# First self attention of a two-layer decoder: output products of tile pairs by seven block products in place of eight

## The chip, the cores and the metric

The kernel runs on one core of a Trainium2 chip. Its time is the device time of one execution in microseconds (us). All matmuls that matter here are in fp32; in the traces each of them shows as two rows of TensorE, each with its own weight load. TensorE is called PE below, VectorE DVE, ScalarE ACT, GpSimd POOL, as the profile does.

## The reference

The input is 8 sequences of 112 tokens of width 512, that is 896 tokens or 7 token tiles of 128. Two decoder layers follow each other, each with self attention, cross attention and a feed-forward part, each behind a layer norm and added to the residual stream `x`. The part that matters is the self attention of the first layer:

```python
q = (x @ Wq + bq).reshape(Bq, Tq, H, D)      # H = 32 heads of D = 64
k = (x @ Wk + bk).reshape(Bq, Tq, KV, D)     # KV = 8
v = (x @ Wv + bv).reshape(Bq, Tq, KV, D)
q = q * cos + _rotate_half(q) * sin          # k likewise
scores = einsum('bhqd,bhkd->bhqk', q, k) * D ** (-0.5)   # causal, window of 64
combined = concatenate([scores, sink_col], axis=-1)
probs = softmax(combined, axis=-1)[..., :-1]
out = einsum('bhqk,bhkd->bhqd', probs, v).reshape(Bq, Tq, H * D)
return out @ Wo + bo
```

The change is in the last product, `out @ Wo`, with `out` of 896 x 2048 and `Wo` of 2048 x 512. The second layer's self attention has the same shape of output product.

## The kernel before

**Turns and units.** `self_attention(layer)` serves both layers. The 2048 rows of `Wo` are four groups `g` of 512 (8 heads of 64 in the first layer); the 8 sequences are two halves `hf` of 4. A turn is one group and one half, in the order of `turns` (turn n is group n // 2, half n % 2). In the first layer a turn has 4 units, one sequence each.

**The pipeline.** `pipeline` runs a turn in two stretches: `weave` mixes the main steps of two units with filler steps, in proportion to their listed costs. The main steps of a unit are two transposes of probabilities (`ppt`), the scores of the unit two ahead (`ps`) and the context product (`po`, written to `oT` by ACT). The first stretch's filler is the preparation of the next turn (`prepare`: one k and four q projections, `pr_k` and `pr_q`, each rotated by `roped`) and the late output products of the turn before. The second stretch's filler is the early output products of this turn and extra steps (biases and the sums of absolute values for the feed-forward weights, `ternary_sum`, L1108). PE's order is the order in which the program emits; it is fixed by hand (`manual_schedule`). The order on the other engines is planned when the kernel is built: of the instructions that are ready, the one earliest in the program goes first. Each engine then works through its own queue in that order and stops at an instruction whose input is missing.

**The output products.** A token tile can be projected when all its tokens have passed `oT`; `completed` says which: of half 0 early tile 0, late tiles 1 and 2; of half 1 early tiles 3 and 4, late tiles 5 and 6. `project_out` runs 4 matmuls of 128 x 512 outputs into one bank of PSUM (`po_at`, L442 and L446) and DVE adds the bank to `x` (L447).

**The seven products.** In the second layer, and there for groups 0 to 2, `outputs` gives a pair of tiles to `out_pair` instead. It takes the product of [2 token tiles x 2 halves of the group's rows] by [2 halves of rows x 2 halves of columns] as a 2 x 2 block product with 7 block products in place of 8 (Strassen's scheme in Winograd's form): each block product is 2 matmuls of 256 columns. `lay` makes the sums of the weight blocks for a group (`wos`, partly in place in the weights; lines 267 to 272), `add_up` those of `oT` (`os`, and one block of `oT` in place; L253 to L258). `sevens` runs the products in the order 1, 6, 2 (`first`) and 5, 7, 3, 4 (`second`) through two banks of PSUM: product 2 is accumulated onto product 1's bank, 3 onto 5's and 4 onto 7's, and between them `put` copies or adds the bank out with DVE into `od` (L768, L771):

```python
        def first():
            ...
            product(1, "x")
            product(6, "y")
            product(2, "x")

        def second():
            ...
            product(5, "y")
            product(7, "z")
            product(3, "y")
            product(4, "z")
```

Two adds into `x` are POOL's (L782, L785). `wos`, `os` and `od` have one buffer each.

**The softmax beside it.** Each unit's scores go through DVE (mask add L463, negated maximum L466), ACT (8 exponentials L469), DVE (reciprocal L472) and POOL (L476). POOL also copies the sinks in (L461). A rotated q takes ACT (bias), two transfers on SP's queue (`turned_q`), POOL (L639), DVE (L640) and POOL (L641).

Of the kernel before, what the change touches and what calls it, by code (L numbers as in the profile page):

```python
# [24 lines left out]
G = 4  # L25
# [68 lines left out]
def _spans(widths):  # L94
    at, out = 0, {}
    for k, n in widths.items():
        out[k] = (at, n)
        at += n
    return out, at
# [58 lines left out]
def decoder(ctx: ExitStack, tc: tile.TileContext, i: dict, out: bass.AP):  # L158
# [9 lines left out]
    def stage_pool(name, side="left"):  # L168

        return tc.alloc_tile_pool(name=name, bufs=2, side=side, reuse_waits="tile")  # L170
# [14 lines left out]
    def weight(src, name, pool=None, tag="w", bufs=None, behind=None):  # L185
        t = (pool or wpool).tile([P, 4, D], F32, tag=tag, bufs=bufs, name=name)
        fetch(t.rearrange("p a b -> p (a b)"), src, behind)
        return t
# [8 lines left out]
    spans, n = _spans(_COLS)  # L197
# [7 lines left out]
    rspans, n = _spans(_ROWS)  # L205
# [12 lines left out]
    def col(name, k):  # L218
        return cols[:, spans[name][0] + k : spans[name][0] + k + 1]
# [55 lines left out]
    def later(steps):  # L275
        return [(0.0, f) for f in steps]
# [109 lines left out]
    def turned_tile(src, xT, k, name, bank=None):  # L386

        pt = (bank or turning)(f"pt_{name}_{k}").rearrange("p (c t) -> p c t", c=NC)
        for c in range(NC):
            nc.tensor.transpose(pt[:, c, :], src[:, c * P : (c + 1) * P], ident)  # L390
        for hf in range(2):
            lo, hi = max(k * P, hf * HT), min((k + 1) * P, (hf + 1) * HT)
            if lo < hi:
                nc.scalar.copy(xT[hf][:, :, lo - hf * HT : hi - hf * HT], pt[:, :, lo - k * P : hi - k * P])
# [20 lines left out]
    def entering(pool, xT, name, tiles, bufs, bank=None):  # L415

        xn = {}

        def norm():
            xn.update(zip(tiles, normed(pool, tiles, name, bufs)))  # L420

        return [(0.0, norm)] + [(0.45, lambda k=k: turned_tile(xn[k], xT, k, name, bank)) for k in tiles]
# [120 lines left out]
    def self_attention(layer, following=None, behind=None, xT=None):  # L543

        l0 = layer == 0
# [5 lines left out]
        dq, wos = [], {}  # L551

        if l0:
            pool, mid, top, tpool = (
                stage_pool("at0"), stage_pool("atm0"), stage_pool("att0"), stage_pool("tern0", "right")
            )
# [23 lines left out]
        else:  # L580
            npool, pool, top = (stage_pool(f"at{t}1", "right") for t in "nmt")
# [6 lines left out]
        def values(b):  # L588
            ps = mm(f"pv{layer}_{b}")
            accumulate(ps[:T, :], [(xT[b // HB][:, c, bcols(b)], wv[:, c, :]) for c in range(NC)])  # L590
            if l0:
                nc.vector.tensor_tensor(v[:, b, :], ps[:T, :], row("bv"), ALU.add)
            else:
                nc.vector.tensor_copy(v[:, b, :], ps[:T, :])
# [26 lines left out]
        def roped(dst, w, at, xh, bias, which, name):  # L621

            cos, sin = (
                const(f"{n}{which}{layer}").unsqueeze(1).to_broadcast([P, HB, T]) for n in ("cos", "sin")
            )
            ps = mm(f"pr_{name}")
            accumulate(ps[:, :HT], [(w[:, c, at : at + P], xh[:, c, :]) for c in range(NC)])
            raw = top.tile([P, HT], F32, tag="raw", bufs=3, name=f"raw_{name}")
            if bias is None:
                nc.vector.tensor_copy(raw, ps[:, :HT])  # L630
            else:
                nc.scalar.activation(raw, ps[:, :HT], AF.Identity, bias=bias)

            turned = top.tile([P, HT], F32, tag="turned", bufs=3, name=f"turned_{name}")
            for at in range(0, P, half):
                other = at ^ half
                issued.append(nc.sync.dma_start(out=turned[at : at + half, :], in_=raw[other : other + half, :]).ins)
            by_batch = lambda t: t.rearrange("p (b t) -> p b t", b=HB)
            nc.gpsimd.tensor_tensor(by_batch(dst), by_batch(raw), cos, ALU.mult)  # L639
            nc.vector.tensor_tensor(by_batch(turned), by_batch(turned), sin, ALU.mult)  # L640
            nc.gpsimd.tensor_tensor(dst, dst, turned, ALU.add)  # L641

        def prepare(n):
            g, hf = turns[n]
            nm = f"{layer}_{g}_{hf}"
            for k in {0: [] if l0 else [0, 1], 1: [0, 1] if l0 else []}.get(n, [g + 1] if hf == 1 and g + 1 < G else []):
                matrices[k] = [
                    wq0 if l0 and m == "q" and k == 0
                    else weight(i[f"{key}_{m}"][k], f"w{m}{layer}_{k}", behind=behind if k == 0 else None)
                    for m in "qo"  # L650
                ]
            wq = wq0 if l0 and g == 0 else matrices[g][0]
            home = mid if hf else top
            kT = home.tile([P, HT], F32, tag="kT", bufs=1, name=f"kT_{nm}")
            qT = home.tile([P, 4, HT], F32, tag="qT", bufs=1, name=f"qT_{nm}")
            held[n].update(kT=kT, qT=qT)
            steps = []
            if l0 and n == 7:
                steps = list(joined[0]["raw"])
            elif n == 1:  # L660
                steps = [(3.4, lambda b=b: values(b)) for b in (2, 3)[1 if l0 else 0 :]]
                if not l0:
                    steps += entering(npool, xT, "at1", [6], 3)
            steps += [(3.0, lambda: roped(kT, wk, g * P, xT[hf], col("bk", g) if l0 else None, "k", f"k_{nm}"))]
            more = later(lay(g - 1)) if not l0 and n and hf == 0 else []
            for c in range(4):
                steps += more[c : c + 1]
                steps.append((3.0, lambda c=c: roped(
                    qT[:, c, :], wq, c * P, xT[hf], col("bq", 4 * g + c) if l0 else None, "q",
                    f"q_{nm}_{c}",  # L670
                )))
            if n == 1:
                steps += [(3.4, lambda b=b: values(b)) for b in (4, 5)]
            if l0 and n == 0:
                for k in range(4, NT):
                    steps.insert(2 * k - 6, (0.45, lambda k=k: turned_tile(xn[k], xT, k, "at0")))
            if l0 and n == 7:
                for k, rope in enumerate(joined[0]["ropes"][:4]):
                    steps.insert(len(steps) - 3 + k, rope)
            return steps  # L680
# [42 lines left out]
        def lay(g):  # L723

            b = matrices[g][1].rearrange("p (h k) (s n) -> p h k s n", h=2, s=2)

            def new():
                wos[g] = dq[0].tile([P, 3, 2, D // 2], F32, tag="wos", bufs=1, name=f"wos_{layer}_{g}")

            return block_differences(  # L730
                (nc.vector, nc.gpsimd), new, lambda k: b[:, 0, :, 1] if k == 2 else wos[g][:, min(k, 2)],
                b[:, 0, :, 0], b[:, 0, :, 1], b[:, 1, :, 0], b[:, 1, :, 1],
            )
# [58 lines left out]
        def outputs(n, late):  # L792
            g, hf = turns[n]
            tiles = completed(hf, late)
            if not l0 and len(tiles) == 2 and g < G - 1:
                return out_pair(g, tiles[0], f"at{layer}_{n}_{late}")
            return [
                (3.4, lambda k=k: project_out(
                    k, [(oT[:, c, k * P : (k + 1) * P], matrices[g][1][:, c, :]) for c in range(4)], f"at{layer}_{n}"
                ))  # L800
                for k in completed(hf, late)
            ]
# [16 lines left out]
        def go():  # L819
            nonlocal oT, late  # L820
            if not l0:
                late = stage_pool("atl1")
                joined.append(following(npool, late))
            if not l0:
                dq.append(stage_pool("dq"))
            oT = (pool if l0 else late).tile([P, 4, NB * T], F32, tag="oT", bufs=1, name=f"oT{layer}")
            pipeline(
                turns, HB if l0 else HB // 2, 2 if l0 else 1, prepare, scores, contexts, outputs, extra,
                begun=None if l0 else 0, finale=finale, between=l0,
                keys_early=(2, 4) if l0 else (),  # L830
            )
            if l0:
                pool.release()
            joined[0]["go"]()
            if not l0:
                for p in (late, pool, npool):
                    p.release()
# [1098 lines left out]
```

## Time and profile before

| | |
|---|---|
| time, median of 3 runs | 1810.11 us (1806.64 to 1810.22) |
| profiled execution | 1806.85 us, span 1804.1 us |
| PE busy | 1758.9 us, 97% |
| DVE busy | 947.0 us, 52% |
| ACT busy | 627.6 us, 35% |
| POOL busy | 799.2 us, 44% |
| 75 to 327 us of the span: PE, DVE, ACT, POOL busy | 251.00, 153.44, 107.46, 132.14 of 252 us |
| granted TensorE clock | 0.999 |

The first self attention's turns lie between about 40 and 345 us of the span. In the lines of the order of time, the first number is the start, the second the length of the merged piece, then engine, line of the source, operation, what is written from what, the shape, and the number of instructions; in brackets stands how long the engine had been idle and what released it. `po_at` is the old projection's bank; `px`, `py` and `pz` are the banks of the seven products; `True` in a name marks a late pair, `False` an early one.

### The profile page before, as it was taken

The numbers are of one execution on the slowest core, as the hardware profiler recorded it, in microseconds if no ns is written. First come the engines' busy times: TensorE is split into PE (matmuls) and PEld (weight loads), VectorE is DVE, ScalarE is ACT, GpSimd is POOL, SyncE is SP. The second block draws the span as 40 slices with busy tenths as digits, with TensorE's granted clock in tenths as the row PEclk, the third lists the DMA queues.
The fourth block names the chain that finished last, engine by engine and source line by source line (L and its number), as shares of the span: only waits on it lengthen the run. The fifth ranks groups of instructions, "written<-read, shape, count | busy, mean of one in ns | idle before, by whom it ended". The sixth has DMA issues, their size and how long they took to land.

```text
span 1804.1 us, 20354 instructions
## 1 busy us (share of the span) xinstructions
PE 1758.9 (97%) x7150; PEld 990.9 (55%) x7150; DVE 947.0 (52%) x1668; ACT 627.6 (35%) x1906; POOL 799.2 (44%) x697
## 2 busy tenths in 40 slices
PE   8999999999999999999999999999999999999998
PEld 4454544555554555567655666655655555555554
DVE  4455666745353544786543455445765444444444
ACT  2444444554333434375321122135733111041110
POOL 3465555355555560000035666621363565535653
PEclk9999999999999999999999999999999999999999
DMA  6132422143223212011221321120011222011101
GB/s 244 27 119 59 148 83 75 76 152 111 53 76 111 59 47 100 19 75 47 70 66 33 86 73 36 39 96 1 2 44 51 60 75 82 24 51 56 63 34 41
DMA packets 40429, 124.50 MB, mean 69 GB/s; under 512 B 7332, under 2 KB 20700, under 8 KB 32904
## 3 DMA queue, kind: packets, MB, share of 16 engines
q1 hardware_dynamic: 33192, 93.73, 16.1%
q0 software_dynamic: 6848, 29.36, 5.5%
q8 instruction: 56, 0.92, 0.2%
q14 instruction: 45, 0.37, 0.1%
q10 hardware_dynamic: 288, 0.12, 0.0%
HBM read 94.56 MB, written 10.28 MB: 58 GB/s over the span
## 4 chain that ended last, share of the span: by engine, by line
PE 87%; DVE 6%; ACT 3%; POOL 1%; SPq 1%; DMA 1%; issue 1%; ACTq 0%; POOLq 0%; DVEq 0%
PE pr_q L244 10%; PE pf L244 6%; PE pb_dn L1550 4%; PE po_x L1004 4%; PE pb_up L1550 4%; PE po_at L442 3%; PE pv L244 3%; PE po_at L446 3%; PE ps L695 3%; PE pr_k L244 3%; PE pq_x L244 3%; PE po L714 3%; PE pg_dn L1550 3%; PE po_x L442 2%; PE po_x L446 2%; PE pg_up L1550 2%
## 5 line engine op out<-in xcount | busy, mean ns | idle before, releaser
L244 PE MATMUL pr_q<-xT_at,wq 128*128 128x448 f32 x512 | 204.1, 543 | 0.0
L244 PEld LDWEIGHTS pr_q<-xT_at,wq 128*128 128x128 f32 x512 | 93.9, 190 | 84.2 <-issue 81.2
L469 ACT ACTIVATE p<-p,nmax 112x113 f32<-112x113 f32 x256 | 95.8, 376 | 109.5 <-DVE nmax L466 108.6
L476 POOL TENSOR_TENSOR p<-p,total 112x896 f32<-112x896 f32 (+1 forms) x56 | 85.3, 1529 | 94.6 <-DVE total L472 87.4
L1736 POOL TENSOR_TENSOR h<-silu,h 128x448 f32<-128x448 f32 x64 | 73.0, 1144 | 95.9 <-ACT silu L1734 95.9
L1127 POOL TENSOR_SCALAR tl<-tr,ternary_bounds 128x512 f32<-128x512 f32 x32 | 51.3, 1603 | 123.3 <-DMA tr<-in_c_w_dram 123.3
L244 PE MATMUL pf<-h,sw 128*128 128x448 f32 x256 | 105.9, 540 | 0.0
L974 DVE TENSOR_REDUCE nmax_x<-ps_x 112x2 f32<-112x750 f32 x64 | 57.2, 934 | 79.1 <-PE ps_x L968 79.1
L639 POOL TENSOR_TENSOR qT<-raw_q,tables 128x448 f32<-128x448 f32 x64 | 86.1, 1350 | 28.0 <-DVE raw_q L630 20.5
L641 POOL TENSOR_TENSOR qT<-qT,turned_q 128x448 f32<-128x448 f32 x64 | 75.2, 1177 | 50.6 <-DVE turned_q L640 41.2
L1004 PE MATMUL po_x<-pT_x,kv 125*128 125x448 f32 x192 | 89.2, 549 | 1.2 <-DVE pT_x L999 0.8
L1550 PE MATMUL pb_dn<-h,sums_dn 128*128 128x448 f32 x192 | 80.2, 540 | 3.4 <-DVE xT_ff L1779 1.7
L976 ACT ACTIVATE p_x<-ps_x,nmax_x 112x375 f32<-112x375 f32 x124 | 69.7, 574 | 38.2 <-DVE nmax_x L974 38.1
L1734 ACT ACTIVATE silu<-pf,cols 128x448 f32<-128x448 f32 x64 | 40.5, 634 | 115.6 <-PE pf L244 114.6
L488 DVE COPY pT<-ppt 112x448 f32<-112x448 f32 x96 | 57.1, 617 | 43.1 <-PE ppt L487 43.0
L469 ACT ACTIVATE p<-ps,nmax 112x112 f32<-112x112 f32 x128 | 43.2, 365 | 102.2 <-DVE nmax L466 102.2
L442 PE MATMUL po_at<-wo,oT 128*128 128x512 f32 x152 | 74.3, 611 | 0.0
L244 PEld LDWEIGHTS pf<-h,sw 128*128 128x128 f32 x256 | 48.5, 190 | 46.5 <-issue 40.1
L446 PE MATMUL po_at<-wo,oT 128*128 128x512 f32 x152 | 71.4, 592 | 0.0
L476 POOL TENSOR_TENSOR p_e<-p_e,total_e 112x896 f32<-112x896 f32 x16 | 26.9, 1682 | 96.5 <-DVE total_e L472 72.2
L719 ACT COPY oT<-po 128x448 f32<-128x448 f32 x64 | 31.9, 524 | 104.8 <-PE po L714 104.8
L995 PEld LDWEIGHTS ppt_x<-consts,p_x 112*125 112x125 f32 x372 | 50.2, 188 | 29.6 <-issue 15.3
(358 smaller groups left out, 3953.7 us busy)
## 6 DMA issues: line engine op xcount, KB each, us to landing
tw<-in_c_w_dram SPq DMA_DIRECT2D x16, 512.0 KB
tr<-in_c_w_dram POOLq DMA_DIRECT2D x32, 256.0 KB, 4.1
signs<-tl POOLq DMA_DIRECT2D x32, 256.0 KB, 2.9
fup<-in_f_up_dram SPq DMA_DIRECT2D x8, 1024.0 KB
fdn<-in_f_dn_dram SPq DMA_DIRECT2D x8, 1024.0 KB
turned_q<-raw_q SPq DMA_DIRECT2D x128, 56.0 KB
turned_q<-raw_q SPq DMA_DIRECT2D x64, 112.0 KB
share<-gated SPq DMA_DIRECT2D x12, 448.0 KB
```

What stands on the lines that cost most here:

```text
L244: nc.tensor.matmul(ps, lhsT, rhs, start=(k == 0), stop=(k == len(pairs) - 1))
L442: nc.tensor.matmul(ps[0], lhsT, rhs, start=(c == 0), stop=False)
L446: nc.tensor.matmul(ps[0], lhsT, rhs, start=False, stop=(c == len(pairs) - 1))
L469: nc.scalar.activation(p[:, h, :], src[:, h, :], AF.Exp, bias=nmax[:, h : h + 1], accum_out=total[:, h : h + 1])
L476: spread[:] = [nc.gpsimd.tensor_tensor(p[:, at, :T], p[:, at, :T], total[:, at], ALU.mult).ins]
L639: nc.gpsimd.tensor_tensor(by_batch(dst), by_batch(raw), cos, ALU.mult)
L641: nc.gpsimd.tensor_tensor(dst, dst, turned, ALU.add)
L974: nc.vector.tensor_reduce(nmax, ps[:T, :, :L], AX.X, ALU.max, negate=True)
L976: e = nc.scalar.activation(p[:, 2 * j + s, :], ps[:T, s, :L], AF.Exp, bias=nmax[:, s : s + 1], accum_out=total[:, 2 * j + s : 2 * j + s + 1],)
L1004: nc.tensor.matmul(po[0][:, : 4 * T], kv[:, b, c, :], pTs[c], start=(c == 0), stop=(c == NLC - 1))
L1550: nc.tensor.matmul(bank[n], lhsT, rhs, start=(k == 0 and n in (1, 6, 7)), stop=(k == len(pairs) - 1), skip_group_check=True,)
L1736: nc.gpsimd.tensor_tensor(to, s, at["h1"][:, c, half(hf)], ALU.mult)
```

## The change

The seven products, so far used in the second layer alone, are used in the first one too: for groups 0, 1 and 2, whenever two tiles come together. `lay` is emitted in the preparation of the next group, `add_up` before the pair's products. The three new tiles `wos`, `os` and `od` lie in the pool `att0` (`top`), which exists in the first layer; group 3 and the single tile 0 of each group are projected as before.

```diff
@@ prepare
-            more = later(lay(g - 1)) if not l0 and n and hf == 0 else []
+            more = later(lay(g - 1)) if n and hf == 0 else []
@@ outputs
-            if not l0 and len(tiles) == 2 and g < G - 1:
+            if len(tiles) == 2 and g < G - 1:
                 return out_pair(g, tiles[0], f"at{layer}_{n}_{late}")
@@ go
-            if not l0:
-                dq.append(stage_pool("dq"))
+            dq.append(top if l0 else stage_pool("dq"))
```

## The prediction

> **What bounds the kernel now.** I read first the busy times on the page, then the chain that ended last, then the order of time on TensorE and VectorE around the projections that the change touches, in the first and in the second self attention.
>
> ```profile
> span 1804.1 us, 20354 instructions
> PE 1758.9 (97%) x7150; PEld 990.9 (55%) x7150; DVE 947.0 (52%) x1668; ACT 627.6 (35%) x1906; POOL 799.2 (44%) x697
> ```
>
> TensorE is the bound. In the windows view the stretch 75 to 327 us, which holds all that changes, has PE busy 251.00 of 252.00 us, VectorE 153.44 and GpSimd 132.14; the chain of waits between 100 and 130 us consists of PE lines alone. So a microsecond of TensorE work taken out there is a microsecond won, and one that TensorE waits is one lost.
>
> What is replaced, and its replacement, both stand in the trace. First, in order of time on PE, two old projections of turn 1 (token tiles 1 and 2):
>
> ```profile
> 108.69 1.04 PE L695 MATMUL ps<-kT,qT 64*112 64x112 f32 x16
> 109.66 1.98 PE L442 MATMUL po_at<-wo,oT 128*128 128x512 f32 x4
> 111.48 1.88 PE L446 MATMUL po_at<-wo,oT 128*128 128x512 f32 x4
> 113.29 0.97 PE L714 MATMUL po<-pT,v 112*64 112x448 f32 x4
> 114.19 1.98 PE L442 MATMUL po_at<-wo,oT 128*128 128x512 f32 x4
> ```
>
> Then a pair of the second self attention, which already uses the seven products (an fp32 matmul shows as two rows, so a product of two matmuls is x4):
>
> ```profile
> 997.82 1.03 PE L286 MATMUL px_at_True<-wo,oT 128*128 128x256 f32 x4
> 998.70 1.13 PE L286 MATMUL py_at_True<-wos,os_at_True 128*128 128x256 f32 x4
> 999.67 1.03 PE L286 MATMUL px_at_True<-wo,oT 128*128 128x256 f32 x4
> ...
> 1003.98 1.74 PE L695 MATMUL ps<-kT,qT 128*112 128x112 f32 x16
> ```
>
> Last, what VectorE does while the first projection of turns 1 and 3 (A pair, then B pair) runs:
>
> ```profile
> 109.78 1.09 DVE L463 TENSOR_TENSOR p<-ps,tables 112x896 f32<-112x896 f32 x1 [0.54 <-PE ps L695]
> 110.78 0.61 DVE L640 TENSOR_TENSOR turned_q<-turned_q,tables 128x448 f32<-128x448 f32 x1
> 111.32 1.09 DVE L466 TENSOR_REDUCE nmax<-p 112x8 f32<-112x904 f32 x1
> ```
>
> ```profile
> 198.97 1.08 DVE L463 TENSOR_TENSOR p<-ps,tables 112x896 f32<-112x896 f32 x1
> 199.97 1.21 DVE L1108 TENSOR_REDUCE ternary_parts<-tw 128x1 f32<-128x1024 f32 x1
> 201.10 1.08 DVE L466 TENSOR_REDUCE nmax<-p 112x8 f32<-112x904 f32 x1
> ```
>
> The planner orders VectorE's queue: whatever is ready goes, earliest in the program first, and a ready instruction slips in between the mask add (L463) and the maximum (L466) that needs it.
>
> **The matmuls (gain).** Nine pairs change: for each of groups 0, 1, 2 one late pair in the odd turn (tiles 1, 2; I call it A), one early pair in the odd turn (tiles 3, 4; B) and one late pair in the even turn (tiles 5, 6; C). Undisturbed, a pair takes 1003.98 - 997.82 = 6.16 us. One old projection takes 3.45 us where the next matmul is of full height (1042.17 to 1045.62), so a pair 6.90; the 3.63 us of turn 1 holds the change to the 64-row context product, which stays. 6.90 - 6.16 = 0.74, nine times: 6.7 us gained. The products follow each other by 0.865 us (6.05 for seven); the other 0.1, between the first two switches of bank, is in the 6.16.
>
> A rule speaks against narrow matmuls: the Trainium skill, "TensorE: Matmul & The Clock Gate", Back-to-back issue gap, gives sustained spacings of about 81 ns at 128 columns and 131 ns at 512. An estimate from it, by a straight line, is 98 ns at 256: 28 rows would be 2.7 us against 2.1 for 16, a loss of 0.6 us a pair. The trace disagrees (0.216 us a row at 256 columns, 3.45/8 = 0.43 at 512), and I go by the trace.
>
> **The new link between TensorE and VectorE (loss).** The old projection ran eight matmuls into one bank and needed VectorE only afterwards. The new one adds product 2 onto the bank of product 1, so product 2 must wait until VectorE has copied product 1 out (L771, 0.42 us); likewise 3 waits for the add of 5, and 4 for the add of 7. The cover is one product, 0.865 us; it is enough when VectorE is free, as at 997.82, where product 2 follows the first by 1.85 us. In the second self attention's early pairs VectorE is at a maximum (1005.75, 1.09 us) and the copy runs at 1007.50: product 2 starts 2.43 us after the first, PE idle 0.52, three times of three.
>
> In the first self attention `first` follows a score product in every pair, so its copy meets the mask add and the maximum. For A and C the add of a turned q (L640) stands between these in all six cases, and both are earlier in the program than the copy. I put the copy behind them: end of the maximum, or of a second turned q just behind it, plus 0.42, less the start of the projection, less 1.85. Turn 1: 112.41 + 0.42 - 109.66 - 1.85 = 1.32. Likewise turn 2 (153.32, 150.50) 1.39; turn 3 (191.25, 187.90) 1.92; turn 4 (231.91, 228.74) 1.74; turn 5 (269.78, 266.15) 2.20; turn 6 (312.84, 309.15) 2.26. Sum 10.8 us. Bounds: 0, if the copy slips in before the maximum and the turned q; about 16, if the sum over the banks behind it is delayed by 0.8 us more in each.
>
> For B no turned q is due, and I let the copy slip in right behind the mask add: turn 1 (mask ends 122.27, projection 119.56) 1.28; turn 3 (200.05, 197.81) 0.81; turn 5 (277.51, 276.30) none. Its second half also follows a score product; there the add of product 5 takes that place and the add of product 7 comes behind the maximum, while product 4 is due 2.60 us after the start: maximum's end + 2 x 0.42 - start - 2.60 gives 1.04 (128.78, 125.98), 1.18 (207.16, 204.22), 0.64 (285.12, 282.72). Sum for B 5.0 us. Every wait of PE holds the context product, the transposes and the next score product behind it by its full length, and a put that waits at the head of VectorE's queue for its product holds the softmax and the turned q behind it, whose users come two units (some 20 us) later. Bounds for B: 0 and 10, the upper end for the eight absolute sums (L1108, 1.22 us each) that lie in turns 1 and 3 beside these pairs, each of which can hold an add up by 1.22 - 0.44 = 0.8.
>
> **Sums and differences beside it (nothing on the path).** Per group `lay` adds three VectorE instructions of 0.68 and one on GpSimd (some 1.27, as the 128x512 add L597); per pair `add_up` adds two on VectorE (0.42) and two on GpSimd (L256 0.96, L258 0.72). That is 9 x 0.84 + 9 x 0.68 = 14 us of VectorE and 9 x 1.68 + 3 x 1.27 = 19 us of GpSimd, over 252 us in which they idle 99 and 120. They are ready early in the turn, where VectorE idles 4.99 us at 105.39 and GpSimd 3.52 at 98.69. If that cover is gone, the last rotated q is late for the next score product: it ended 1.3 to 5.9 us ahead of it in turns 1 to 6. GpSimd's adds into x (L782 0.79, L785 1.27, 18 us in all) lie behind the products; from them waits the copy of the next pair, since `od` has one buffer. For B that is due some 2.9 us after A's last product starts to be counted and I reckon the adds done 2.7 us after it: no cost, up to 1 us for each of three. VectorE's puts replace 18 adds of 0.69 by 63 of 0.42, +14 us, whose cost is the waits above. No DMA is added; the weights `wo` are loaded as before and freed in the same turn, and the larger pool `att0` moves addresses only.
>
> The added VectorE instructions of `lay` and `add_up` read two SBUF inputs, and the trace shows such ones slowed beside GpSimd (L640 0.62 in the median, 3.19 at most; L271 0.66 and 1.65). The Trainium skill, "GPSIMD Engine Reference", Key points, says that the two share SBUF interfaces in just that case. By an estimate from it all 14 us would be taken from GpSimd, which its 120 idle us hold.
>
> **Sum.** -6.7 + 10.8 + 5.0 = +9.1 us. The profiled execution took 1806.85 us (span 1804.1, and 2.75 around it), so 1816.0 by its own time. The median of the runs is 1810.11, which gives 1819.2; two runs lie near 1810 and one with the profile near 1806.7, so I take the middle, 1818.
>
> **Rivals.**
> 1. *TensorE's gain stays (faster).* The copy of product 1 slips in ahead of the turned q or the maximum, as the absolute sum does at 199.97. For it: product 1 ends 1.03 us after its start, before the mask add does. Against: the turned q is ready and earlier in the program in six cases of six. Then -6.7 with between none and all of B's second halves (+2.9): the middle is -5, 1804 by the same middle of the runs. It decides once all waits together stay under 6.7 us, that is, with fewer than four waits of the mean size of A and C (1.8).
> 2. *VectorE runs full (clearly slower).* In turn 3 it is busy 10.95 of the 10.95 us beside the B pair, and puts are added there; the absolute sums fill the 0.44 us holes between puts. Upper bounds: -6.7 + 16 + 10 = +19, 1828.
> 3. *Gain and waits cancel.* The A and C waits come out near 1 us, B's near 0.5: -6.7 + 6 + 3, between -3 and +3 us, about 1810.
>
> **How the numbers follow.** The forecast (+4 to +15) has 0.56, rival 1 0.22, rival 3 0.12, rival 2 0.10. About 0.2% (3.6 us) is what a measurement of this kernel can tell from no change. Faster: rival 1 and little of rival 3, 0.23; within: 0.10; slower: 0.67. The range goes from 1803, in rival 1, to 1827, short of rival 2's end. The likeliest case alone holds 1813 to 1824.
>
> **What would show it.** PE's busy time falls by some 7 us, yet the span grows; PE rows on px (L286) wait for VectorE's copy of `od` (L771), 1 to 2 us each for A and C; VectorE runs mask, turned q, maximum, copy in that order. If the order is mask, copy, maximum, I am wrong and rival 1 holds. If the waits sit on the score products for q, GpSimd was the step that I missed.

## The result and the profile after

The changed kernel takes 1827.44 us (median of 4 runs, 1822.44 to 1828.74) against 1809.86 us (4 runs, 1806.64 to 1810.22) before: ratio 1.0094, 95% interval 1.0074 to 1.0114, 17.6 us slower. The prediction, 1818 with a range to 1827, had the direction and about half of the loss. The profiled execution took 1828.74 us. Its page:

```profile
span 1826.3 us, 20735 instructions
PE 1763.1 (97%) x7258; PEld 1011.3 (55%) x7258; DVE 985.7 (54%) x1740; ACT 627.7 (34%) x1906; POOL 837.2 (46%) x736
```

From before, the span has grown by 22.2 us, VectorE's work by 38.7 and GpSimd's by 38.0. PE is not less busy but 4.2 us more, against the prediction; rows at a halved clock, shown below, count as busy. The largest of PE's new waits (total, times, longest, in us):

```profile
PE px_at_True L286 <- DVE od_at_True L771: 10.2, 6, 2.5
PE px_at_False L286 <- DVE od_at_False L771: 4.1, 6, 1.3
```

The first line is the six late pairs: product 2 waits for the copy of product 1. (Three of the six in the second line are the second layer's, 0.5 each, as before.) In order of time on VectorE and then on PE, the late pair of turn 1:

```profile
112.02 1.09 DVE L463 TENSOR_TENSOR p<-ps,tables 112x896 f32<-112x896 f32 x1 [0.53 <-PE ps L695]
113.03 0.61 DVE L640 TENSOR_TENSOR turned_q<-turned_q,tables 128x448 f32<-128x448 f32 x1
113.56 1.09 DVE L466 TENSOR_REDUCE nmax<-p 112x8 f32<-112x904 f32 x1
114.56 0.41 DVE L771 COPY od_at_True<-px_at_True 128x256 f32<-128x256 f32 x1
...
118.22 1.22 DVE L1107 TENSOR_REDUCE ternary_parts<-tw 128x1 f32<-128x1024 f32 x1 [1.57 <-DMA tw<-in_c_w_dram]
...
119.47 0.37 DVE L768 TENSOR_TENSOR od_at_True<-od_at_True,py_at_True 128x256 f32<-128x256 f32 x1
```

```profile
111.90 1.13 PE L286 MATMUL px_at_True<-wo,oT 128*128 128x256 f32 x4
112.87 1.03 PE L286 MATMUL py_at_True<-wos,os_at_True 128*128 128x256 f32 x4
115.03 1.13 PE L286 MATMUL px_at_True<-wo,oT 128*128 128x256 f32 x4 [1.14 <-DVE od_at_True L771]
...
119.98 0.45 PE L286 MATMUL py_at_True<-wo,os_at_True 128*128 128x256 f32 x1 [0.99 <-DVE od_at_True L768]
```

The queue has exactly the predicted order: mask, turned q, maximum, copy. So it has in turns 2 to 5; in turn 6 a second turned q and three instructions of the next stage (L906 to L908) stand ahead of the copy too. The second half of this pair shows what was not priced: the add of product 5 (119.47) stands behind an absolute sum (L1107) that itself waits for its transfer, VectorE idles 1.57 us, and PE waits once more, before product 3 (the view ends at 120 us, so the last line shows one of its four rows).

The early pair of turn 3, VectorE and then PE:

```profile
202.73 1.88 DVE L253 TENSOR_TENSOR os_at_False<-oT 128x256 f32<-128x256 f32 x1
204.53 1.21 DVE L1107 TENSOR_REDUCE ternary_parts<-tw 128x1 f32<-128x1024 f32 x1
205.66 0.41 DVE L768 TENSOR_TENSOR od_at_True<-od_at_True,pz_at_True 128x256 f32<-128x256 f32 x1
205.99 0.61 DVE L488 COPY pT<-ppt 112x448 f32<-112x448 f32 x1
206.52 0.41 DVE L257 TENSOR_TENSOR os_at_False<-os_at_False,oT 128x256 f32<-128x256 f32 x1
```

```profile
204.89 1.13 PE L286 MATMUL px_at_False<-wo,oT 128*128 128x256 f32 x4
206.99 1.13 PE L286 MATMUL py_at_False<-wos,os_at_False 128*128 128x256 f32 x4 [0.97 <-DVE os_at_False L257]
208.85 1.13 PE L286 MATMUL px_at_False<-wo,oT 128*128 128x256 f32 x4 [0.73 <-DVE od_at_False L771]
```

Here product 6 waits for a token sum: the first of the two sums took 1.88 us instead of the second's 0.41, beside GpSimd, which is busy without a gap from 201.28 to 206.02; the second comes behind it and three others. In the whole first self attention the 18 token sums of VectorE take 19.6 us, where the prediction reckoned 9 x 0.84 = 7.6.

Where the 22.2 us of this execution lie, by the length of each pair on PE against 7.17 us (late) or 7.26 us (early) before; a pair that nothing disturbs takes 2.79 + 3.56 = 6.35 us (seen undisturbed in the experiments below):

| part | us |
|---|---|
| nine pairs at 6.35 us | -7.7 |
| late pairs, first halves, over 2.79 (1.40, 1.83, 1.47, 1.83, 2.50, 3.83) | +12.9 |
| early pairs, first halves, over 2.79 (0.86, 2.23, 2.32) | +5.4 |
| early pairs, second halves, over 3.56 (0.69, 1.36, 0.69) | +2.7 |
| late pair of turn 1, second half | +1.8 |
| last two late pairs, second halves | +1.9 |
| outside the pairs | +5.2 |

The row before the last, about 1 us of the last first half and some 1.6 us outside the pairs are TensorE's clock. The windows view (busy time of PE, PEld, DVE, ACT and POOL; clock, DMA share, GB/s), right after the two longest waits, 2.15 and 2.54 us:

```profile
282.00:284.00 2.00, 2.00 (x6) 0.30 (x5) 0.70 (x2) 2.00 (x12) 1.13 (x1) 0.55 0.26 66
284.00:286.00 2.00, 2.00 (x7) 1.58 (x6) 0.00 (x0) 0.55 (x2) 0.00 (x0) 0.60 0.32 95
330.00:335.00 5.00, 4.37 (x10) 2.06 (x11) 2.51 (x6) 2.63 (x13) 4.28 (x4) 0.50 0.90 338
```

Rows of 256 columns take 0.43 us there instead of 0.216, for 3.4 us the first time and 6.8 the second: at most (3.4 + 6.8) / 2 = 5.1 us. Without them the growth is about 17 us, close to the medians' 17.6. Of the rest outside the pairs, 1.1 us lies in the first 17 us, ahead of everything that the change touches, and 1.1 at 53 us.

### The profile page after: what moved, and what is told of

Read it like the earlier page. It is cut to its first block, busy times and chain, and to the rows that moved or that the text cites. A ratio compares the mean times of both kernels' runs of the same rounds, so it can differ in the third digit from the quotient of the medians.

```text
span 1826.3 us, 20735 instructions
## 1 busy us (share of the span) xinstructions
PE 1763.1 (97%) x7258; PEld 1011.3 (55%) x7258; DVE 985.7 (54%) x1740; ACT 627.7 (34%) x1906; POOL 837.2 (46%) x736
## 4 chain that ended last, share of the span: by engine, by line
PE 71%; DVE 6%; ACT 3%; POOL 2%; issue 1%; DMA 0%; SPq 0%; POOLq 0%; ACTq 0%; DVEq 0%
PE pf L244 6%; PE pr_q L244 5%; PE pb_dn L1549 4%; PE po_x L1003 4%; PE pb_up L1549 3%; PE pq_x L244 3%; PE pg_dn L1549 2%; PE po_x L442 2%; PE po_x L446 2%; PE pg_up L1549 2%; PE pa_up L1549 2%; PE pa_dn L1549 2%; PE ps_x L967 2%; PE po_ff L1244 2%; PE ph L244 2%; PE ppt_x L994 2%
## 5 line engine op out<-in xcount | busy, mean ns | idle before, releaser
L695 PEld LDWEIGHTS ps<-kT,qT 64*112 64x112 f32 (+1 forms) x768 | 56.5, 178 | 17.1 <-issue 8.5
L695 PE MATMUL ps<-kT,qT 64*112 64x112 f32 (+1 forms) x768 | 62.4, 269 | 2.3 <-POOL qT L641 2.3
```

What stands on the lines that cost most here:

```text
L695: nc.tensor.matmul(ps[:T, 4 * k + h, :T], qT[at, h, bcols(b)], kT[at, bcols(b)], start=True, stop=True)
```

## The experiments

In each, the time before is that of the same chip: 1809.13 us for the first four runs, 1808.07 for the next four, 1807.82 for the last four. Waits and starts are those of one profiled execution.

**1. The copy on ScalarE.**

```diff
-                    nc.vector.tensor_copy(d1, ps)
+                    (nc.scalar.copy if l0 else nc.vector.tensor_copy)(d1, ps)
```

> The copy of product 1 out of its bank runs on ScalarE in the first self attention (nine copies), all else as in the changed kernel. Queue theory (PE waits because the copy stands behind a turned q and the maximum in VectorE's queue): the six waits of A and C, 10.2 us in the changed kernel's profile, fall below 0.3 us each, the clock stays whole through 270 to 345 us, and the time is 2 to 6 us above before, where the changed kernel is 17.6 above. Load theory (the added sums and puts crowd VectorE and GpSimd as a whole): nine copies of 0.42 us less on VectorE change little, 13 to 18 us above before.

Measured: 1831.31 us, ratio 1.0120 (1.0101 to 1.0139), +22.2, more than either theory had. Five of the six copy waits are gone, the sixth grew to 4.3 us (the copy now stood in ScalarE's queue), and in their place query products wait 3.7 us in all for ScalarE's raw q, and products of the early pairs 3.7 us for VectorE's adds. Moving the copy to another engine removed the waits that the profile named, and as much came back under other names.

**2. The puts first on VectorE.** Same operations and engines, other order: mask, copy, turned q, add, maximum.

```diff
-            first, second = sevens(products, put, D // 2, nm)
+            def early_put(n, ps):
+                with tc.high_priority() if l0 else nullcontext():
+                    put(n, ps)
+
+            first, second = sevens(products, early_put, D // 2, nm)
```

> No instruction is added, removed or moved to another engine: the planner only gets the pair's copies and adds out of the banks with a higher priority, so that VectorE's queue runs mask add, copy, turned q, add, maximum. Queue theory: waits of A and C below 0.3 us each, clock whole, 2 to 6 us above before. Load theory: unchanged, 13 to 18 us above before. If the softmax behind it becomes late instead, PE waits show on the transposes of p.

Measured: 1819.6 us, ratio 1.0060 (1.0045 to 1.0075), +10.5. Four late pairs (turns 2 to 5) are now undisturbed or within 0.1 us of it, which confirms queue position as the cause of their waits. But 10.5 us remain, between the two theories: the copy of turn 6 still waits 2.1 us, turn 1's second half loses 1.7 us to the absolute sum's transfer as in the changed kernel, and the early pair behind it 3.7. Another part, VectorE and then ScalarE ahead of the late pair of turn 3:

```profile
181.41 1.32 DVE L253 TENSOR_TENSOR os_at_True<-oT 128x256 f32<-128x256 f32 x1 [0.73 <-ACT oT L719]
182.76 1.24 DVE L257 TENSOR_TENSOR os_at_True<-os_at_True,oT 128x256 f32<-128x256 f32 x1
183.92 1.08 DVE L463 TENSOR_TENSOR p<-ps,tables 112x896 f32<-112x896 f32 x1
184.92 1.92 DVE L640 TENSOR_TENSOR turned_k<-turned_k,tables 128x448 f32<-128x448 f32 x1
186.77 1.08 DVE L466 TENSOR_REDUCE nmax<-p 112x8 f32<-112x904 f32 x1
```

```profile
187.94 0.39 ACT L469 ACTIVATE p<-p,nmax 112x113 f32<-112x113 f32 x1 [6.04 <-DVE nmax L466]
...
190.94 0.61 ACT L632 ACTIVATE raw_q<-pr_q,cols 128x448 f32<-128x448 f32 x1
```

The two token sums, stretched to 1.3 us, stand ahead of the mask, and a turned k, stretched to 1.9 us, behind it; the maximum is late by them, then the eight exponentials, and behind these in ScalarE's queue the raw q, whose bank the next query product needs: PE waits 1.57 us. The sums are not "beside" the path; their victim is two engines away.

**3. Late pairs alone** (tiles 3 and 4 projected as before, but from weights in which one block is already replaced).

```diff
-            if len(tiles) == 2 and g < G - 1:
+            if len(tiles) == 2 and g < G - 1 and (late or not l0):
```

> Only the late pairs (A and C, six) take the seven products; tiles 3 and 4 are projected one by one as before. Queue theory: A and C keep their waits (10.2 us), B's net cost in the changed kernel (5.4 us from the lengths of its rows) goes: 8 to 14 us above before. Buffer theory (what costs is that B follows A at once and shares os, od and the banks with it): 0 to 3 us above before.

Measured: 1820.66 us, ratio 1.0066 (1.0042 to 1.0090), +11.5, of which the copy waits are 9.4 us: the queue theory, by its number. So the early pairs cost about 6 us of the 17.6 (the interval of this run alone leaves some 4 us either way), where the prediction's terms gave them 5.0 - 2.2 = 2.8.

**4. The sums alone**, all tiles projected as before; the differences and token sums go into tiles that nothing reads.

```diff
             if len(tiles) == 2 and g < G - 1:
-                return out_pair(g, tiles[0], f"at{layer}_{n}_{late}")
+                steps = out_pair(g, tiles[0], f"at{layer}_{n}_{late}")
+                if not l0:
+                    return steps
+                sums = steps[:1]
```

> The sums of the weight blocks and of oT are made for all nine pairs as in the changed kernel (into tiles of their own, nothing in place) and nobody reads them; all tiles are projected as before. It prices the step that I put at nothing. Queue theory: 0 to 3 us above before, the sums planned at 40 us costing about 1. Load theory: 8 us or more above before.

Measured: 1817.89 us, ratio 1.0054 (1.0033 to 1.0076), +8.8. PE's new wait is for the probabilities, which GpSimd multiplies (1.1 us before):

```profile
PE ppt L487 <- POOL p L476: 5.2, 4, 3.3
```

This is the step of the prediction that failed: it had the sums and differences at nothing.

**5. A filler product in the wait** of the late pairs (one 128x512 product, read by nothing), so that TensorE idles less before product 2.

```diff
             product(6, "y")
+            if fill:
+                fill()
             product(2, "x")
```

> One extra 128x512 product (read by nothing) stands between products 6 and 2 of each of the six late pairs, so that TensorE is not idle for the whole of the copy's wait; the sums, the pairs and the order on VectorE stay as in the changed kernel. An estimate from this case's rows: the filler lasts 0.86 us (two passes of 0.43), so waits of 1.1 to 2.5 us become 0.3 to 1.7 us of idling, none longer than the 1.8 us after which the clock stayed whole. Theory A (the two longest waits make the granted clock fall to 0.5, and that costs about 5 us apart from the waits themselves): about +12 us against the kernel before (+9 to +14), no row of 427 ns in the first layer. Rival (the clock's dips cost nothing that repeats; the waits are the whole loss): +17 to +19, as without the filler, or more by what the filler lengthens.

Measured: 1824.69 us, ratio 1.0102 (1.0083 to 1.0122), +16.6. The idle times before product 2 fell to 0.28 to 1.69 us and the profiled execution has no halved stretch after a late pair; it is 17.1 us behind where the first self attention ends. That is near the rival's 17 to 19 and well above theory A's 9 to 14: the clock cost one execution some 5 us, not the median. Run 12 below shows the same without a filler.

**6. The weights' differences alone.** As run 4, without the token sums.

> All tiles are projected as before the change; only the weights' differences (four 128x512 operations for each of three groups: three on VectorE, one on GpSimd) are made, into a tile that nothing reads. The token sums are left out. Theory A (the differences wait for nobody, but others wait for them: the first group's stand ahead of the first masks, 1.2 us late at 53 us, the second group's ahead of a probability product on GpSimd, 3.3 us): +3 to +7 us, more than half of the +8.8 of the run with all sums. Rival B (the token sums carry nearly all of it): 0 to +2. What the prediction said of this step: 0.

Measured: 1812.02 us, ratio 1.0019 (1.0008 to 1.0030), +4.0, so the token sums are about the other half of the 8.8, if the two add up. VectorE's queue at the second group's differences, and the probability product on GpSimd:

```profile
129.30 0.69 DVE L267 TENSOR_TENSOR wos<-wo 128x512 f32<-128x512 f32 x1 [1.67 <-DMA wo<-in_a_o_dram]
129.91 1.08 DVE L463 TENSOR_TENSOR p<-ps,tables 112x896 f32<-112x896 f32 x1
130.91 0.19 DVE L472 RECIPROCAL total<-total 112x8 f32<-112x8 f32 x1
131.18 3.15 POOL L476 TENSOR_TENSOR p<-p,total 112x896 f32<-112x896 f32 x1
```

The first difference is at the head of the queue before its weights have landed; VectorE idles 1.67 us, and behind it wait a mask and the reciprocal of the unit before. GpSimd's probability product, which needs that reciprocal, then takes 3.15 us instead of 1.68 beside the other differences, and PE waits 2.3 us for it. The first group's differences do the same to the first two masks (1.77 us of idling at 39.54, PE 1.2 us late at 53 us). That half is in the changed kernel too (1.35 us at 39.99); the second is not, since there the second group's tile comes free only at 165 us. So the sums alone overstate what they cost beside the products.

**7. Token sums behind the maximum.** As run 2, and the late pairs' token sums are issued only behind the score maximum (and emitted two filler steps later).

```diff
-                    step()
+                    with tc.issue_after(reduced[0]) if l0 and nm.endswith("True") else nullcontext(): step()
```

> The eviction of the first product goes first (as in the run with the puts first, +10.5 us), and the token sums of the six late pairs are issued only behind the score maximum that follows them on VectorE. Same operations, other order. Theory A (what is left of the loss is queue position: the two sums, stretched to 1.2 to 1.3 us each beside GpSimd, stand ahead of a mask, so the maximum, eight exponentials and then raw_q on ScalarE are late, and the next query product waits 1.6 us, twice): +4 to +8 us against before, no wait of over 0.6 us for raw_q at the third and fifth turn's end. Rival B (VectorE and GpSimd have no room for the sums wherever they stand): +9 to +12, the wait only changes its name.

Measured: 1817.56 us, ratio 1.0061 (1.0047 to 1.0075), +9.5. Rival B, by its number: the query product ahead of the late pair is 0.8 us late instead of 2.1, but the copies of turns 3 and 5 are 0.6 to 0.7 us late again. In turn 3 they now stand behind an absolute sum for whose transfer VectorE idles 1.86 us. One tight place gave way to the next.

**8. Late pairs, differences in tiles of their own and behind the maximum.** Else as run 7.

```diff
-            if len(tiles) == 2 and g < G - 1:
+            if len(tiles) == 2 and g < G - 1 and (late or not l0):
...
-                wos[g] = dq[0].tile([P, 3, 2, D // 2], F32, tag="wos", bufs=1, ...)
+                wos[g] = [top.tile([P, 2, D // 2], F32, tag="xn", bufs=4, ...) for k in range(4)]
...
+                with tc.issue_after(reduced[0]) if l0 and reduced else nullcontext():
+                    step()
```

> As the run before it, and two things more: only the six late pairs are made by seven products (tiles 3 and 4 are projected as before), and the weights' differences go into tiles of their own (four that held the normalised input, by then dead) and are issued behind a score maximum instead of ahead of the first masks. Six pairs can save 0.74 us each, 4.4 us in all. If everything that was late was a matter of position: -4 to 0 against before. If the sums cost by their load: +3 to +7. My middle: +2.

Measured: 1813.06 us (12 runs), ratio 1.0026 (1.0015 to 1.0037), +5.0. The delay at 53 us is gone. In the trace this kernel runs 1.1 us ahead of before until its last pair, and level with it where the first self attention ends. Its profiled execution loses most of its 6 us later, in stages that nobody changed: 1.7 us each in two stretches of halved clock (granted 0.52 at 1257 to 1260 us, 0.62 at 1347 to 1350) and 1.8 us at a wait for VectorE at 1515 us. Much of the median's 5 us goes with the clock as well: eight of these twelve executions have a mean granted clock of 0.996 or less, and only two of the 22 of the kernel before. Whether the change brings those halvings about is not settled by this.

**9. Four of those six pairs**, without the first and the last.

```diff
-            if len(tiles) == 2 and g < G - 1 and (late or not l0):
+            if len(tiles) == 2 and g < G - 1 and (not l0 or late and 0 < n < 5):
```

> As the run with late pairs and tiles of their own (+5.0 us by the medians, but 1.1 us ahead of the kernel before where the trace leaves the first layer), without the first and the last of its six pairs: those two stood behind a ternary sum that waits for its transfer (1.4 us) and behind the next stage's work (1.2 us). Four pairs at 6.35 to 6.6 us instead of 7.17 save 2.3 to 3.3 us; the differences and token sums cost 0 to 1. Expected where the first layer ends: 2 to 3 us ahead of before. By the medians: -3 to +2, middle -1; if what that run lost behind the first layer (three halvings of the clock, 1.4 to 1.8 us each) belongs to it and is not chance, +2 to +4.

Measured: 1805.22 us (11 runs, 1803.05 to 1807.78) against 1807.82 us (23 runs): ratio 0.9987 (0.9978 to 0.9996), 2.6 us faster than the kernel before. It is the only version here that beats the kernel before. Its pairs (6.35, 6.35, 6.35 and 6.51 us) have no wait, as in turn 2, VectorE and then PE:

```profile
150.29 1.09 DVE L463 TENSOR_TENSOR p<-ps,tables 112x896 f32<-112x896 f32 x1 [0.72 <-PE ps L695]
151.30 0.41 DVE L783 COPY od_at_True<-px_at_True 128x256 f32<-128x256 f32 x1
```

```profile
150.10 1.13 PE L286 MATMUL px_at_True<-wo,oT 128*128 128x256 f32 x4
151.07 1.03 PE L286 MATMUL py_at_True<-wos,os_at_True 128*128 128x256 f32 x4
151.93 1.03 PE L286 MATMUL px_at_True<-wo,oT 128*128 128x256 f32 x4
```

The copy stands right behind the mask and ends 0.2 us before product 2 is due. At the context product inside the last of the four, the trace is 3.1 us ahead of before (0.4 of it from the first 17 us), one unit later 2.6. It stays 2.8 ahead up to 323 us; then a stretch of halved clock (granted 0.50 at 328 to 330 us) costs 1.5 us, and this execution ends only 0.7 us ahead. That the medians differ by 2.6 us as well is thus partly chance.

**10. Products without sums** (for all nine pairs).

> The seven products and their eight additions for all nine pairs, but with unsummed blocks as operands: the weights' differences and the token sums are left out, so the output isn't the reference's. Theory A (two losses that add up: sums +8.8 us by themselves, and copies in VectorE's queue): 17.6 - 8.8, about +9 us (+6 to +12), waits for the copy of 1.1 to 2.5 us still there. Rival B (the copies are late only because the sums crowd VectorE): -3 to +2.

**11. The same with the puts first.**

> As the run before it (weights' differences and token sums left out, unsummed blocks as operands, output not the reference's), and with the puts given priority on VectorE. Only the saved matmuls and the puts' own work are left: 9 times 0.74 us saved, against 1.4 us at the first pair, about 1.2 at the last, and some 0.2 in each early pair. Theory A (queue position and sums are all of the loss): -5 to -1 us against before. Rival B (additions on VectorE cost wherever they stand): +3 to +7.

Measured: run 10, 1821.35 us, ratio 1.0071 (1.0054 to 1.0088), +13.5; run 11, 1810.27 us, ratio 1.0014 (1.0003 to 1.0025), +2.5. Run 10 is above theory A's range and far from rival B: the copies wait 8.5 us without any sum nearby. Run 11 falls between its two theories; its trace is 1.2 us behind before where the first self attention ends, 0.7 of it from the first 17 us, having lost what the matmuls saved at the first pair (1.7 us, the absolute sum's transfer again), the early pairs (1.3, then 0.1 and 0; second halves 0.5 to 0.7 each) and the last pair. With the changed kernel and run 2 they make a square (us against before, by medians):

| | puts where the planner put them | puts first |
|---|---|---|
| without sums | +13.5 | +2.5 |
| with sums | +17.6 | +10.5 |

The place of the puts costs 11.0 without sums and 7.1 with them; the sums cost 4.1 or 8.0. By the intervals, the 8.0 is clear of zero and the 4.1 is not; the traces support it, since without the sums the first halves of the early pairs lose 2.1 us in place of 5.4, and the 1.1 us at 53 us is gone. The two overlap; that a softmax which is late catches up while PE waits for a copy is the likely reason, not tried by itself.

**12. Two buffers for the token sums and the partial products.**

> The changed kernel with two buffers each for the token sums and for the partial products, so that a pair never waits until the pair before it, and its GpSimd addition, have let go of them (the weights' differences move to tiles that the normalised input had). Theory A (the early pairs' waits of 0.6, 1.7 and 1.8 us are partly these buffers: GpSimd's release ended 0.44 us of one): +14 to +16 us against before. Rival B (they wait for the place of the sums and of the copy in VectorE's queue): +16.5 to +19, no change.

Measured: 1825.98 us, ratio 1.0107 (1.0090 to 1.0125), +18.2: rival B, no buffer is missing. And this run shows the loss without the clock: its profiled execution has the same two long waits (2.15 and 2.55 us before product 2), and the stretch behind the second at full clock:

```profile
330.00:335.00 5.00, 5.00 (x23) 3.31 (x22) 3.38 (x8) 1.69 (x8) 4.38 (x5) 1.00 0.94 385
```

It is nevertheless 18.1 us behind where the first self attention ends. Two of its executions have a mean granted clock of 1.000 and take 1823.7 us; the five such of the kernel before have a median of 1805.8, 17.9 less. The loss is in the waits.

## Why the prediction was right and wrong

- *Matmuls, -6.7.* Right: an undisturbed pair saves 0.82 (late) or 0.91 us (early), 7.7 in all instead of 6.7.
- *Late pairs' copies, +10.8.* Right in mechanism and size, and in the order but for turn 6's three extra instructions: 1.14, 1.56, 1.21, 1.57, 2.15 and 2.54 us, 10.2 in all, against 1.32, 1.39, 1.92, 1.74, 2.20 and 2.26. Rival 1 fell with it. The restart after each wait, which the sum left out, adds some 0.26 us (1.40 against 1.14 in turn 1).
- *Early pairs, +5.0.* Mis-sized: 8.1 us. The second halves, 2.7, agree with the reckoned 2.9; the first halves came to 5.4 instead of 2.1, because in turns 3 and 5 product 6 waits for a token sum, or for an add behind two of them, and these were priced as free. Without the sums they still come to 2.1 (0.78, 1.23, 0.13 in run 10), the very number reckoned, though by luck: pair by pair it was 1.28, 0.81 and 0.
- *Absolute sums.* They stood only in the upper bound, at 0.8 us each, by their own length. What happened in turn 1 is worse and rarer: the one at the head waited for its transfer, and an add behind it cost 1.8 us.
- *Sums and differences, "nothing on the path".* This is the step that failed: +8.8 us alone, 4.1 on top of the products. The argument was 99 idle us of VectorE and 120 of GpSimd against 14 and 19 of new work. But a queue is served in order, and idle time elsewhere does not move a mask or a probability product forward. Nor did the lengths hold: the token sums took 19.6 us of VectorE in place of 7.6, and the trace before already had one of them at 0.83 us in the second layer's early pairs. The victim named for lost cover, the last rotated q, was the wrong one: no score product waits for it in the changed kernel that did not before. The late ones were the softmax (maximum, exponentials, product on GpSimd) and, behind the exponentials, ScalarE's raw q.
- *GpSimd's adds into x, none to 1 us.* Right: VectorE's copy waits for them once, 0.44 us in turn 1, and two buffers win nothing.
- *Rival 2* came closest by its number, 1828, but only by adding its own upper bounds: 16 us for the late pairs' copies, where 10.2 were measured, and 10 for the early pairs, where it was 8.1. It had nothing for the sums.
- *PE's busy time falls by 7.* Wrong as a mark: it rose by 4.2 us, and with the clock whole (run 12) fell by 2.3. The length of a pair from first row to next matmul showed the gain, the busy sum did not.

So, roughly, +9.1 became +17.6: 4.1 by the sums (the square), 1.8 by the transfer in turn 1, 1.6 by six restarts, less 1.0 that the matmuls gave more and 0.8 by which the waits for puts came out shorter; the remaining 2.8 us lie in the last pair and outside the pairs and were not taken apart.

## What to carry to other kernels

When a change trades work of a full engine for work of a half-idle one, do not weigh busy sums: list, for each added instruction, what stands behind it in its queue until the next product is due, and follow that to the engine that feeds the full one. A link that makes the full engine wait for another within a microsecond paid here only where the answer could go to the head of that queue: four places out of nine had that, and taking those alone, with the side work put behind the softmax, turned 17.6 us of loss into 2.6 us of gain (0.7 to 4.0 by the interval). Test a step priced at nothing by doing it alone.

## What the hardware showed that was not expected

TensorE's granted clock fell to 0.50 after waits of 2.15 and 2.54 us in one execution, for 3.4 and 6.8 us, and stayed at 1.00 after the same waits in another. It also fell after shorter ones: to 0.50 at 209 us of run 5, behind waits of 0.97 and 0.73 us, and at 328 us of run 9, amid waits of 1.10, 0.61 and 0.65 us that the kernel before has too, at full clock. The Trainium skill, "TensorE: Matmul & The Clock Gate", What's actually happening, gives half rate after at least one idle window of about 3.4 us; these gaps were shorter, so the trace disagrees on the length, though the halved stretches of the changed kernel are one and two times 3.4 us long. A halving costs some 1.7 us for each 3.4 us, and the mean granted clock changes between executions of one kernel (0.995 to 1.000 in the 23 of the kernel before on one chip), so that one profile must not be read as the median.

VectorE's two-input sums of 128x256 took 0.42 us alone and up to 1.88 beside GpSimd, and GpSimd's probability product 3.15 us instead of 1.68 beside VectorE's differences. The prediction's estimate had GpSimd alone pay; here both engines did.
